# Stationary operands of a GRU scan interleaved in pairs, weight blocks displaced by some bytes

## Chip, cores and metric

The kernel runs on one core of a Trainium2 chip. The metric is the device time of one execution in microseconds, here the median of a few runs. Each profile is of one execution.

## The reference

Two stages, each added to its input. The first is a GRU over 64 steps (batch 128, width 512) followed by a linear layer with ternary weights; the second is a causal convolution and a mixture of experts. The change touches the first, which is

```python
def cell(h, x):
    gi = x @ W_ih + b_ih
    gh = h @ W_hh + b_hh
    i_r, i_z, i_n = jnp.split(gi, 3, axis=-1)
    h_r, h_z, h_n = jnp.split(gh, 3, axis=-1)
    r = jax.nn.sigmoid(i_r + h_r)
    z = jax.nn.sigmoid(i_z + h_z)
    n = jnp.tanh(i_n + r * h_n)
    h_new = (1.0 - z) * n + z * h
    return (h_new, h_new)
...
x = x + linear(scan(cell, cond_2048, x), ternary(weight)) + bias
x = x + moe(causal_conv(x, cond_2048) + b)
```

All inputs and outputs are float32.

## The kernel before

Time steps run one after the other. In each, x and h (128 rows of batch by 512) lie transposed: four k tiles of 128 features by 128 rows of batch. A product with a 512 x 512 block of weights is four matmuls that add up in one bank of PSUM: the k tile of x or h is the **stationary** operand (128 columns, loaded by an LDWEIGHTS of its own), and the four rows of the weight block (512 columns each) are the **moving** one. `products` (L337) issues such four.

To keep float32's precision with the faster type float32r, each operand is split in three: a part `h` with the low bits cut off, the rest `l`, and a mixture `s`. So one gate takes three products: h with h, l with l into one bank, s with s into another. Tiles of x are called xh, xl, xs, those of the state hh, hl, hs; the weights wih0 to wih2 and whh0 to whh2 (gates r, z, n), each in three planes; sgn is the ternary weight of the linear layer, multiplied with hh and hl only. In a settled step there are therefore 9 groups of four for x, 9 for h and 2 for sgn: 80 matmuls, and 4 transposes of h.

The order on TensorE in a step: wih2 and wih0 of the next step's x, the four transposes of h (`turned_up`, L418), wih1 of x, then the state's groups whh0h, whh2h, whh0l, whh0s, whh2l, whh2s, whh1 (three), then sgn for the state before.

The splitting: `masked` (L349) cuts the low bits on VectorE into `cut` (hcut from PSUM, xcut from SBUF), ScalarE casts it to the part h (L380, L436), and `low_parts` (L354) makes l (GpSimd for x from step 4 on, else VectorE) and s (VectorE). `late_ffn` (L563) does the same for four early steps whose linear layer is put off. Between them VectorE and ScalarE compute the gates (`cell_r`, `cell_n`, `cell_z`).

Memory: pools on the left grow from the low end (edge with `scale`, el0 with the tiles of x, wh0 to wh2 with whh, sgn), pools on the right from the high end (few, wi with wih, xp with the tiles of h). `scale` and `few` are made larger than needed by LEFT_PAD and RIGHT_PAD (in words of 4 bytes). By their sizes, all float32r tiles of the scan then begin at the same place modulo 1024 bytes.

Of the kernel before, what the change touches and what calls it, by code (L numbers as in the profile page):

```python
# [8 lines left out]
F32 = mybir.dt.float32  # L9
# [3 lines left out]
F32R = mybir.dt.float32r  # L13
# [6 lines left out]
P = 128  # L20
B = 128
T = 64
D = 512
KD = D // P
# [11 lines left out]
SPLIT = 4096.0  # L36
LOW = -4096
WHOLE = 1.0 + 1.0 / SPLIT
LEFT_PAD = 216
RIGHT_PAD = 504  # L40
DOWN_PAD = 216


# [5 lines left out]
def adaln_ffn_kernel(  # L49
# [22 lines left out]
    nc = tc.nc  # L72
# [51 lines left out]
    def clear(i):  # L124
        nc.gpsimd.memset(tzs[i], 0.0)
# [86 lines left out]
    with (  # L212
# [7 lines left out]
        br, bz, bin_, bhn, fb = (w0.tile([P, D], F32, name=n) for n in ("br", "bz", "bin", "bhn", "fb"))  # L220
        scale = edge.tile([P, LEFT_PAD], F32, name="scale")[:, :1]

        wi_ = ExitStack()
        few = wi_.enter_context(tc.tile_pool(name="few", bufs=1, side="right")).tile(
            [P, RIGHT_PAD], F32, name="few"
        )
        ones, part = few[:, :P], few[:, P : P + T]
        total, half, nhalf = (few[:, n : n + 1] for n in range(P + T, P + T + 3))
        wi = wi_.enter_context(tc.tile_pool(name="wi", bufs=1, side="right"))
        xpp = wi_.enter_context(tc.tile_pool(name="xp", bufs=2, side="right"))  # L230

        def planes(pool, name):
            return [pool.tile([P, KD, D], F32R, name=f"{name}{n}") for n in "hls"]

        wih = [planes(wi, f"wih{c}") for c in range(3)]
        wh0 = ExitStack()
        whh = [planes(wh0.enter_context(tc.tile_pool(name="wh0", bufs=1)), "whh0"), None, None]

        stage = ExitStack()
        st = stage.enter_context(tc.tile_pool(name="st", bufs=1))  # L240
# [12 lines left out]
        xps, xns, parts_of = {}, {}, {}  # L253
# [6 lines left out]
        LATE = 4  # L260
# [15 lines left out]
        def load_for(step):  # L276

            load_x(step - 1)
            t = postponed.get(step)
            if t is not None:  # L280
                load_x(t)
                hts[t] = slot()
                nc.gpsimd.dma_start(out=hts[t], in_=htd[t])
# [17 lines left out]
        h = el0.tile([P, D], F32, name="h")  # L301
# [25 lines left out]
        ps = ps_f.tile([P, D], F32, name="psf")  # L327
# [5 lines left out]
        def banks(c):  # L333
            pool = ps_gh if c == 1 else ps_gi
            return [pool.tile([P, D], F32, name=n) for n in BANKS[c]]

        def products(ps, lhs, rhs, start=False, stop=False):  # L337
            for k in range(KD):
                i = nc.tensor.matmul(  # L339
                    ps,  # L340
                    lhs[:, k, :],
                    rhs[:, k, :],
                    start=start and k == 0,
                    stop=stop and k == KD - 1,
                    skip_group_check=True,
                )
            return i

        def masked(dst, src):  # L349
            return nc.vector.tensor_scalar(  # L350
                dst.bitcast(I32), src.bitcast(I32), LOW, None, ALU.bitwise_and
            )

        def low_parts(engine, lo, mix, full, cut):  # L354

            i = engine.tensor_sub(lo, full, cut)  # L356
            nc.vector.scalar_tensor_tensor(mix, lo.bitcast(F32), -SPLIT, cut, ALU.mult, ALU.add)  # L357
            return i

# [13 lines left out]
        def split_x(t):  # L373

            xp = xps.pop(t)
            cut = xpp.tile([P, KD, B], F32, name="xcut", bufs=1)
            parts_of[t] = [el0.tile([P, KD, B], F32R, name=f"x{n}") for n in "hls"]
            xh, xl, xs = parts_of[t]
            masked(cut, xp)
            nc.scalar.copy(xh, cut)  # L380
            return low_parts(nc.vector if t < LATE else nc.gpsimd, xl, xs, xp, cut)

        gis = {}

# [40 lines left out]
        def place(t, n):  # L425

            if t < T - TAIL:
                return xpp.tile([P, KD, B], F32R, name=f"h{n}", bufs=1)
            return el0.tile([P, KD, B], F32R, name=f"x{n}")

        def split_h(ps, t, mixed=True):

            cut = el0.tile([P, KD, B], F32, name="hcut")
            hh, hl, hs = (place(t, n) for n in "hls")
            masked(cut, ps)
            nc.scalar.copy(hh, cut)  # L436
            if mixed:
                low_parts(nc.vector, hl, hs, ps, cut)
            else:
                nc.vector.tensor_sub(hl, ps, cut)  # L440
            return hh, hl, hs

        last = []
# [39 lines left out]
        def cell_r(t, ps):  # L483
            a, b = ps
            r = el0.tile([P, D], F32, name="rz")
            if t == 0:
                nc.vector.tensor_add(r, b, br)
            else:
                nc.vector.scalar_tensor_tensor(r, a, WHOLE, br, ALU.mult, ALU.add)
                nc.vector.tensor_add(r, b, r)  # L490
            nc.scalar.activation(r, r, AF.Sigmoid)  # L491
            return r
# [29 lines left out]
        for c in (0, 2, 1):  # L522
            a, b = banks(c)
# [14 lines left out]
        r = cell_r(0, first[0])  # L538
        n = cell_n(0, (None, first[2][1]), r)
# [23 lines left out]
        def late_ffn(t):  # L563

            hh, hl = (place(t, n) for n in "hl")
            cut = el0.tile([P, KD, B], F32, name="hcut")
            full = hts.pop(t).rearrange("p (k b) -> p k b", k=KD)
            masked(cut, full)
            nc.scalar.copy(hh, cut)
            nc.vector.tensor_sub(hl, full, cut)  # L570
            ffn(t, (hh, hl))

        split_x(1)
# [8 lines left out]
        for t in range(1, T):  # L582
            if t > LATE and t + 2 <= T:
                load_for(t + 2)
            if t + 2 < T:
                load_xt(t + 2)
            if 2 <= t < 2 * NSL + 2:
                toeplitz(t - 2)

            gates = [state_gate(t, c, pieces, hT) for c in (0, 2, 1)]  # L590
            next(gates[0])
            next(gates[1])
            ps_r, ps_n = next(gates[0]), next(gates[1])
            next(gates[2])
            ps_z = next(gates[2])
            if t + 1 < T:
                last_low = split_x(t + 1)
            if t > LATE:
                add_bias(t + 1, last_low)
            r = cell_r(t, ps_r)  # L600
            n = cell_n(t, ps_n, r)
            cell_z(t, ps_z, n)
            if t == LATE:
                ternary(wf)
                more.append(wi.tile([P, KD, D], F32, name="q"))
                for n in range(1, 3):
                    load_for(t + n)
                add_bias(t + 1)
            if t > LATE:
                ffn(t - 1, pieces)  # L610
            if t + 1 < T:
                pieces, hT = next_inputs(t)
            if t in (1, 2):
                c = 3 - t
                whh[c] = planes(
                    wh0.enter_context(tc.tile_pool(name=f"wh{c}", bufs=1, reuse_waits="tile")),
                    f"whh{c}",
                )
                with tc.tile_pool(name="cuts", bufs=2, reuse_waits="tile") as cuts:
                    convert(raw_h[c], whh[c], cuts)  # L620
                if t == 1:
                    late_.close()
                else:
                    sgn = wh0.enter_context(
                        tc.tile_pool(name="sgn", bufs=1, reuse_waits="tile")
                    ).tile([P, KD, D], F32R, name="sgn")
                    wf = wi.tile([P, KD, D], F32, name="q")
                    load_rows(wf, wfT)
            if t == T - TAIL:
                wi_.close()  # L630
                cb = conv.enter_context(
                    tc.tile_pool(name="cb", bufs=1, side="right", reuse_waits="tile")
                ).tile([P, D], F32, name="cb")
                for i in range(NCB):
                    conv_buffers(i)
                    clear(i)
                tail = conv.enter_context(
                    tc.tile_pool(name="tail", bufs=1, side="right", reuse_waits="tile")
                )
                xl = tail.tile([P, TAIL, D], F32, name="xl")  # L640
                tap = tail.tile([P, TAIL, D], F32, name="tap")
                load_piece(0)
                repeated(cb, cbias)
                for i in range(1, NCB):
                    load_piece(i)
                for j in range(TAIL):
                    nc.gpsimd.dma_start(out=tap[:, j], in_=cond[B - 1 - j].partition_broadcast(P))
                last += [xl, tap]
# [31 lines left out]
    xl, tap = last  # L680
# [19 lines left out]
    with tc.tile_pool(name="ps_c", bufs=4, space=PSUM) as ps_c:  # L700
        for sl in range(NSL):
# [6 lines left out]
            for g in range(DS // 4):  # L708
                if early:
                    ps = early.pop(0)  # L710
                else:
                    ps = conv_group(sl, g, ps_c.tile([P, D], F32, name="psc"))
# [33 lines left out]
    full = SI // P  # L746
# [963 lines left out]
    for i in range(NI // 2 + 1, NI):  # L1710
        n = i - NI // 2 - 1
# [64 lines left out]
```

## Time and profile before

| | us |
|---|---|
| median of 3 runs | 2439.01 (2437.75 to 2439.14) |
| the profiled execution | 2436.07 |
| its span, first to last instruction | 2434.0 |
| TensorE busy | 2420.9 (99%) |
| weight loads busy | 1866.9 (77%) |
| VectorE busy | 1579.1 (65%) |
| mean granted TensorE clock | 1.000 |

PE is TensorE's matmuls, PEld its weight loads, which overlap them; DVE is VectorE, ACT ScalarE, POOL GpSimd, SP the queue of SyncE. A timeline's line gives start and length in us, engine, line of the kernel, operation, result and inputs by the program's names, shapes (a moving operand of float32r is shown as f32 like any other) and how many instructions were merged; in brackets stands the idle time of the engine ahead of it and what ended it. Lengths of matmuls include their way through the array, so that consecutive ones overlap: the pace is read from the starts. Lines of groups give, behind the first bar, the busy time in us and the mean of one instruction in ns, and behind the second the engine's idle time ahead of them and what ended it.

The scan takes about the first 1207 us of the span. A settled step takes 18.63 us, from one set of transposes (start 505.55) to the next.

### The profile page before, as it was taken

To read this page: it belongs to the slowest core of one execution; us is meant where nothing else is said; L and a number is where in the kernel's file an instruction comes from. 1 tells how busy PE (TensorE), PEld (TensorE's weight loads), DVE (VectorE), ACT (ScalarE), POOL (GpSimd) and SP (SyncE) were. 2 spreads that over 40 slices of the span, in tenths; PEclk is the share of its full clock that TensorE was granted. 3 is DMA by queue.
4 is the path that set the end of the run, shared out by engine and by line. 5 is a ranking of instruction groups with operands and counts; after the bars stand their busy time and mean duration, and the time that the engine had idled before them with its cause. 6 is when DMAs were issued, how large, how long until landed. Compare 5 with 4: busy or idle time off the path is not lost.

```text
span 2434.0 us, 32114 instructions
## 1 busy us (share of the span) xinstructions
PE 2420.9 (99%) x12221; PEld 1866.9 (77%) x12221; DVE 1579.1 (65%) x3116; ACT 492.7 (20%) x900; POOL 447.2 (18%) x468
## 2 busy tenths in 40 slices
PE   9999999999999999999999999999999999999999
PEld 5788888888888888888896777777776666676667
DVE  8977777777777777777687766666753333343344
ACT  5211111111111111111123333233311111111111
POOL 1222221121112111211220000000012222222220
PEclk9999999999999999999999999999999999999999
DMA  5244443333232222222498123343459999899961
GB/s 188 80 85 82 80 81 59 67 66 63 57 61 57 57 54 59 60 53 48 130 344 291 29 40 75 98 113 92 135 147 288 296 297 304 268 321 307 286 180 34
DMA packets 469096, 330.71 MB, mean 136 GB/s; under 512 B 317136, under 2 KB 384720, under 8 KB 466768
## 3 DMA queue, kind: packets, MB, share of 16 engines
q1 hardware_dynamic: 439904, 254.47, 36.9%
q0 software_dynamic: 28896, 73.95, 12.9%
q8 instruction: 96, 1.57, 0.3%
q14 instruction: 56, 0.46, 0.1%
q10 hardware_dynamic: 144, 0.26, 0.0%
HBM read 241.83 MB, written 92.03 MB: 137 GB/s over the span
## 4 chain that ended last, share of the span: by engine, by line
PE 97%; DVE 1%; DMA 1%; issue 1%; ACT 0%; POOL 0%; DVEq 0%; ACTq 0%; POOLq 0%
PE psa L339 9%; PE psw L339 9%; PE psx L339 9%; PE psw L830 7%; PE psz L830 7%; PE psx L830 7%; PE psb L339 5%; PE psz L339 5%; PE psy L339 5%; PE psf L339 5%; PE py L1661 3%; PE y L830 3%; PE pg L1635 3%; PE pu L1635 3%; PE y L1006 2%; PE y L1098 2%
## 5 line engine op out<-in xcount | busy, mean ns | idle before, releaser
L1645 DVE SCALAR_TENSOR_TENSOR a<-a,rw,pu 128x352 f32<-128x352 f32 x32 | 18.6, 580 | 213.1 <-PE pu L1635 213.1
L357 DVE SCALAR_TENSOR_TENSOR xs<-xl,xcut 128x512 fp32r<-128x512 f32 x63 | 103.4, 1641 | 65.6 <-POOL xl L356 65.6
L1193 POOL DMA_DIRECT2D out_dram<-hid x60 | 53.4, 1075 | 493.5 <-DVE hid L1125 372.0
L830 PE MATMUL psx<-hid,sw 128*128 128x256 f32 x512 | 132.3, 381 | 0.0
L350 DVE TENSOR_SCALAR hcut<-pst 128x512 int32<-128x512 int32 x63 | 43.5, 691 | 130.1 <-PE pst L422 128.4
L356 POOL TENSOR_TENSOR xl<-xp,xcut 128x512 fp32r<-128x512 f32 x60 | 83.3, 1389 | 144.6 <-PE psa L339 131.7
L491 ACT ACTIVATE rz<-rz 128x512 f32<-128x512 f32 x64 | 40.5, 633 | 334.1 <-DVE rz L490 333.1
L830 PEld LDWEIGHTS psx<-hid,sw 128*128 128x128 f32 x512 | 94.3, 190 | 15.3 <-issue 2.9
L436 ACT CAST hh<-hcut 128x512 fp32r<-128x512 f32 x61 | 37.9, 621 | 325.0 <-DVE hcut L350 325.0
L272 POOL DMA_DIRECT2D q<-in_x_dram x36 | 19.3, 537 | 410.1 <-DMA out_dram<-q 328.1
L1661 PE MATMUL py<-wd,aeT 128*64 128x512 f32 (+1 forms) x288 | 88.7, 595 | 0.0
L830 PE MATMUL psw<-hid,st 128*128 128x256 f32 x320 | 83.1, 382 | 0.1
L1635 PE MATMUL pg<-wg,hid 128*64 128x352 f32 x384 | 81.1, 459 | 0.0
L1635 PE MATMUL pu<-wu,hid 128*64 128x352 f32 x384 | 81.1, 459 | 0.0
L1672 POOL DMA_INDIRECT out_dram<-hid,idxp x32 | 46.4, 1449 | 179.6 <-DMA out_dram<-hid,idxo 92.3
L1672 POOL DMA_INDIRECT out_dram<-hid,idxo x32 | 45.4, 1418 | 172.3 <-DMA out_dram<-hid,idxp 152.2
L870 ACT ACTIVATE g<-psx 128x256 f32<-128x256 f32 x80 | 30.8, 384 | 218.4 <-DVE aT L877 157.5
L504 ACT ACTIVATE n<-n 128x512 f32<-128x512 f32 x64 | 40.5, 633 | 166.6 <-DVE n L503 166.6
L339 PE MATMUL psa<-wih1h,xh 128*128 128x512 f32 x252 | 74.2, 415 | 0.0
L830 PE MATMUL y<-hid,st 128*128 128x256 f32 x280 | 74.0, 381 | 0.0
L272 POOL DMA_DIRECT2D xn<-in_x_dram x28 | 15.0, 537 | 318.6 <-DMA out_dram<-xn 269.5
L830 PE MATMUL psz<-hid,st 128*128 128x256 f32 x280 | 72.4, 380 | 0.0
(432 smaller groups left out, 6214.6 us busy)
## 6 DMA issues: line engine op xcount, KB each, us to landing
wg<-in_w_gate_dram SPq DMA_DIRECT2D x48, 704.0 KB, 12.7
wu<-in_w_up_dram SPq DMA_DIRECT2D x48, 704.0 KB, 13.4
wd<-in_w_down_dram SPq DMA_DIRECT2D x48, 512.0 KB, 10.8
xc<-x1c SPq DMA_DIRECT2D x32, 512.0 KB, 6.1
xp<-in_xT_dram POOLq DMA_DIRECT2D x62, 256.0 KB, 2.9
out_dram<-hid POOLq DMA_DIRECT2D x60, 256.0 KB, 5.2
tab<-hid SPq DMA_DIRECT2D x56, 256.0 KB, 5.0
hid<-in_w_gate_dram SPq DMA_DIRECT2D x16, 704.0 KB, 8.7
```

The lines of the kernel that those rows point to most:

```text
L339: i = nc.tensor.matmul(ps, lhs[:, k, :], rhs[:, k, :], start=start and k == 0, stop=stop and k == KD - 1, skip_group_check=True,)
L350: return nc.vector.tensor_scalar(dst.bitcast(I32), src.bitcast(I32), LOW, None, ALU.bitwise_and)
L356: i = engine.tensor_sub(lo, full, cut)
L357: nc.vector.scalar_tensor_tensor(mix, lo.bitcast(F32), -SPLIT, cut, ALU.mult, ALU.add)
L491: nc.scalar.activation(r, r, AF.Sigmoid)
L830: i = nc.tensor.matmul(ps.rearrange("p (j b) -> p j b", b=P) if len(r.shape) == 3 else ps, lhs(k), r, start=(first and k == 0), stop=(k == ...
L1006: nc.tensor.matmul(gu.rearrange("p (j b) -> p j b", b=P), swr[:, k].rearrange("p w n -> p (w n)"), rows[:, k], start=(k == 0), stop=(k == ...
L1098: nc.tensor.matmul(ps, aparts[n][:, c, steps], dparts[n][:, c], start=c == 0 and n != 1, stop=c == full - 1 and n != 0, skip_group_check=True,
L1193: nc.gpsimd.dma_start(out=out_t[t], in_=rows_of(i)[:, t % NB], accum_op=ALU.add)
L1635: nc.tensor.matmul(acc[halves[j]], self.xeT[:, k, halves[j]], self.ws[j][which][:, k, :], start=(k == 0), stop=(k == KD - 1),)
L1661: nc.tensor.matmul(py[halves[j]], self.aeT[:n, c, halves[j]], self.ws[j][2][:n, c, :], start=(c == 0), stop=(c == len(ech) - 1),)
L1672: nc.gpsimd.indirect_dma_start(out=out, out_offset=bass.IndirectOffsetOnAxis(ap=(idxp[:CAP] if j == 0 else idxo)[:, q : q + 1], axis=0), i ...
```

## The change

Tiles of x, of h and of their cuts are declared as 128 x 2 x 128 x 2 in place of 128 x 4 x 128: tiles k = 0 and 1 lie interleaved, column by column, and so do 2 and 3. A stationary operand's 128 columns are then 8 bytes apart, in place of 4. `apart` gives the view in the old order for writing, and `like` gives a plain source the same four dimensions. What reads and writes interleaved tiles only (the cast, the mixture) stays contiguous.

Unused tiles are placed between the weight blocks: 32 bytes behind wih0, 64 behind wih1, 160 behind wih2, and 64 ahead of each of whh0, whh2, whh1 and sgn. LEFT_PAD and RIGHT_PAD shrink by 64 words, the sum of these on each side.

```diff
-LEFT_PAD = 216
-RIGHT_PAD = 504
+LEFT_PAD = 152
+RIGHT_PAD = 440
...
-        wih = [planes(wi, f"wih{c}") for c in range(3)]
+        def shift(pool, name, words):
+            pool.tile([P, words], F32, name=name)
+
+        wih = []
+        for c, words in enumerate((8, 16, 40)):
+            wih.append(planes(wi, f"wih{c}"))
+            shift(wi, f"gap{c}", words)
         wh0 = ExitStack()
-        whh = [planes(wh0.enter_context(tc.tile_pool(name="wh0", bufs=1)), "whh0"), None, None]
+        wh0p = wh0.enter_context(tc.tile_pool(name="wh0", bufs=1))
+        shift(wh0p, "gap", 16)
+        whh = [planes(wh0p, "whh0"), None, None]
...
+        def paired(pool, name, dtype=F32R, **kw):
+
+            return pool.tile([P, KD // 2, B, 2], dtype, name=name, **kw)
+
+        def apart(pair):
+            return pair.rearrange("p m b r -> p m r b")
+
+        def like(ap):
+            return ap.rearrange("p (m r) b -> p m r b", r=2)
+
         def products(ps, lhs, rhs, start=False, stop=False):
             for k in range(KD):
                 i = nc.tensor.matmul(
                     ps,
-                    lhs[:, k, :],
+                    lhs[:, k, :] if len(lhs.shape) == 3 else lhs[:, k // 2, :, k % 2],
                     rhs[:, k, :],
...
-            i = engine.tensor_sub(lo, full, cut)
+            i = engine.tensor_sub(apart(lo), full, apart(cut))
             nc.vector.scalar_tensor_tensor(mix, lo.bitcast(F32), -SPLIT, cut, ALU.mult, ALU.add)
...
-            cut = xpp.tile([P, KD, B], F32, name="xcut", bufs=1)
-            parts_of[t] = [el0.tile([P, KD, B], F32R, name=f"x{n}") for n in "hls"]
+            cut = paired(xpp, "xcut", F32, bufs=1)
+            parts_of[t] = [paired(el0, f"x{n}") for n in "hls"]
             xh, xl, xs = parts_of[t]
-            masked(cut, xp)
+            masked(apart(cut), like(xp))
             nc.scalar.copy(xh, cut)
...
                 c = 3 - t
-                whh[c] = planes(
-                    wh0.enter_context(tc.tile_pool(name=f"wh{c}", bufs=1, reuse_waits="tile")),
-                    f"whh{c}",
-                )
+                whp = wh0.enter_context(
+                    tc.tile_pool(name=f"wh{c}", bufs=1, reuse_waits="tile")
+                )
+                shift(whp, "gap", 16)
+                whh[c] = planes(whp, f"whh{c}")
```

`place`, `split_h` and `late_ffn` get the same rewriting as `split_x`, and sgn a gap of 16 words in its pool.

More of the change, by code (lines that the diff above doesn't have):

```diff
@@ L375, in split_x @@
             xp = xps.pop(t)
-            cut = xpp.tile([P, KD, B], F32, name="xcut", bufs=1)
-            parts_of[t] = [el0.tile([P, KD, B], F32R, name=f"x{n}") for n in "hls"]
+            cut = paired(xpp, "xcut", F32, bufs=1)
+            parts_of[t] = [paired(el0, f"x{n}") for n in "hls"]
             xh, xl, xs = parts_of[t]
-            masked(cut, xp)
+            masked(apart(cut), like(xp))
             nc.scalar.copy(xh, cut)
-            return low_parts(nc.vector if t < LATE else nc.gpsimd, xl, xs, xp, cut)
+            return low_parts(nc.vector if t < LATE else nc.gpsimd, xl, xs, like(xp), cut)
         gis = {}
@@ L427, in place @@
             if t < T - TAIL:
-                return xpp.tile([P, KD, B], F32R, name=f"h{n}", bufs=1)
-            return el0.tile([P, KD, B], F32R, name=f"x{n}")
+                return paired(xpp, f"h{n}", bufs=1)
+            return paired(el0, f"x{n}")
         def split_h(ps, t, mixed=True):
-            cut = el0.tile([P, KD, B], F32, name="hcut")
+            cut = paired(el0, "hcut", F32)
             hh, hl, hs = (place(t, n) for n in "hls")
-            masked(cut, ps)
+            masked(apart(cut), like(ps))
             nc.scalar.copy(hh, cut)
             if mixed:
-                low_parts(nc.vector, hl, hs, ps, cut)
+                low_parts(nc.vector, hl, hs, like(ps), cut)
             else:
-                nc.vector.tensor_sub(hl, ps, cut)
+                nc.vector.tensor_sub(apart(hl), like(ps), apart(cut))
             return hh, hl, hs
@@ L565, in late_ffn @@
             hh, hl = (place(t, n) for n in "hl")
-            cut = el0.tile([P, KD, B], F32, name="hcut")
+            cut = paired(el0, "hcut", F32)
             full = hts.pop(t).rearrange("p (k b) -> p k b", k=KD)
-            masked(cut, full)
+            masked(apart(cut), like(full))
             nc.scalar.copy(hh, cut)
-            nc.vector.tensor_sub(hl, full, cut)
+            nc.vector.tensor_sub(apart(hl), like(full), apart(cut))
             ffn(t, (hh, hl))
@@ L623, in adaln_ffn_kernel @@
                 else:
-                    sgn = wh0.enter_context(
+                    sgp = wh0.enter_context(
                         tc.tile_pool(name="sgn", bufs=1, reuse_waits="tile")
-                    ).tile([P, KD, D], F32R, name="sgn")
+                    )
+                    shift(sgp, "gap", 16)
+                    sgn = sgp.tile([P, KD, D], F32R, name="sgn")
                     wf = wi.tile([P, KD, D], F32, name="q")
```

## The prediction

> **What bounds the kernel now.** I read the page first, then the weight loads and matmuls one shape apart, then the timeline of one step of the scan, then the timeline of a later stage for comparison. The page:
>
> ```profile
> PE 2420.9 (99%) x12221; PEld 1866.9 (77%) x12221; DVE 1579.1 (65%) x3116; ACT 492.7 (20%) x900; POOL 447.2 (18%) x468
> ...
> PE 97%; DVE 1%; DMA 1%; issue 1%; ACT 0%; POOL 0%; DVEq 0%; ACTq 0%; POOLq 0%
> ```
>
> TensorE is never free and owns 97% of the chain that ended last, so only its pace counts. The timeline of one step, in start and length (us):
>
> ```profile
> 506.19 0.69 DVE L350 TENSOR_SCALAR hcut<-pst 128x512 int32<-128x512 int32 x1 [2.41 <-PE pst L422]
> ...
> 506.91 0.62 ACT L436 CAST hh<-hcut 128x512 fp32r<-128x512 f32 x1 [6.21 <-DVE hcut L350]
> 506.91 0.69 DVE L356 TENSOR_TENSOR hl<-pst,hcut 128x512 fp32r<-128x512 f32 x1
> ...
> 508.53 0.87 PEld L339 LDWEIGHTS psx<-whh0h,hh 128*128 128x128 f32 x4
> 508.76 1.07 PE L339 MATMUL psx<-whh0h,hh 128*128 128x512 f32 x4
> ...
> 510.35 0.87 PEld L339 LDWEIGHTS psx<-whh0l,hl 128*128 128x128 f32 x4
> ```
>
> And ten groups later in the same step, and in the late stage at 2003 us:
>
> ```profile
> 518.73 1.07 PE L339 MATMUL psw<-wih2h,xh 128*128 128x512 f32 x4
> ```
>
> ```profile
> 2003.42 1.03 PE L830 MATMUL psx<-hid,sw0first 128*128 128x256 f32 x4
> 2004.28 1.03 PE L830 MATMUL y<-hid,st 128*128 128x256 f32 x4
> 2005.15 0.49 PE L1650 MATMUL py<-ident,a 128*128 128x128 f32 x3
> ```
>
> From start 508.76 to start 518.73 lie 44 matmuls: 226.6 ns from one to the next. From 2003.42 to 2005.15 lie 8: 216.3 ns. The first kind (float32r, 512 columns) and the second (float32, 256 columns, taking twice the time for a column) keep the array busy for the same number of column times, and the granted clock is 1.0 in both. So the scan's matmuls lose 10.3 ns each that the others don't.
>
> **What the two kinds differ in.** Each matmul runs beside the weight load of the next:
>
> ```profile
> L194 PEld LDWEIGHTS psc<-tz,xc 128*64 128x64 f32 x960 | 55.7, 200 | 2.8 <-issue 2.8
> ...
> L339 PEld LDWEIGHTS psx<-whh0l,hl 128*128 128x128 f32 x244 | 45.8, 188 | 9.5
> ...
> L1239 PEld LDWEIGHTS lg<-hid,gw 128*64 128x64 f32 x256 | 17.8, 137 | 11.1 <-issue 2.8 <-DVE hid L1225 0.3
> ```
>
> The last number ahead of the second bar is the mean of one load. Contiguous loads take 137 ns for 64 columns and 188 for 128: 51 ns for 64 more, 102 ns for the 128. A load therefore reads its 512 bytes of a partition at some 5.0 bytes/ns. The float32 matmul reads 1024 bytes in 216 ns, 4.7 bytes/ns: nearly equal speeds, no loss. The float32r matmul reads 2048 bytes in that time, 9.5 bytes/ns, so the two read streams slide past each other, and this kind loses. I infer that the two streams get in each other's way in the memory when one overtakes the other; no row shows it directly.
>
> **The change, part by part.**
>
> *Interleaving the stationary columns.* A load now spreads 128 columns over 1024 bytes: at 102 ns, 10 bytes/ns, the speed of the moving stream. If what is lost comes from sliding, it goes. The pace in the changed state is in no row, so I bound it: below by the float32 row, 216.3 ns; above by charging the 10.3 ns to the 16-byte pieces that a load touches, 32 now and 64 then: 20.6 ns lost, 236.9. I take 218, near the equal-speed row, leaving 1.7 ns for the start of each load. The float32r matmuls of L339 whose stationary operand changes are nine groups of 252, six of 244, three of 240 and two of 248: 4948. At 226.6 - 218 = 8.6 ns each this is 42.6 us. At the bounds: -51.0 us and +51.0 us.
>
> *The load itself.* If strided columns load more slowly, it may no longer hide. The only strided row is L194, 64 bytes apart: 63 ns more for 64 columns. Doubled for 128 that is 126 ns more, 228 ns of reading instead of 102, which would set a pace of 228: 1.4 x 4948 = 7 us lost. At 8 bytes two columns share a 16-byte piece, so half of the extra, 63 ns, is the nearer estimate: 165 ns of reading, still inside 216. I take nothing.
>
> The Trainium skill, "SBUF — State Buffer", Specifications, asks for at least two hits on each 16-byte line for full bandwidth; 8 bytes gives exactly two. Its page "TensorE: Matmul & The Clock Gate", Step-by-step, speaks against the change: loading the next weights is said not to steal read bandwidth from the running matmul, as the two have separate ports. By that nothing would be gained and the sum would stay at 2439; the 226.6 against 216.3 above does not fit it.
>
> *Displaced weight blocks.* Against the stationary tiles, and counted modulo 256 bytes, the moving blocks now begin 0 (wih0, sgn), 32 (wih1), 64 (whh0), 96 (wih2), 128 (whh2) and 192 bytes (whh1) further; before, all began at the same place. With equal speeds this distance stays fixed through a load, so it may decide. No row shows another distance. Of the 80 matmuls in a step 20 (12 of wih0, 8 of sgn) have distance 0; if only those collide, at +10.3 ns, and the rest gain 10.3, the sum is 4948 x 10.3 x (60 - 20)/80 = 25 us gained.
>
> *The first matmuls behind the transposes.* From 505.90 to 508.76 twelve matmuls take 2.86 us, 0.14 more than 12 x 226.6; some 0.09 of it is the first pair of loads. The other 0.05 x 62 steps = 3 us: I take 2 of them.
>
> *Splitting with strides.* Per step VectorE's hcut, hl, xcut, GpSimd's xl read or write with an 8-byte step. A strided write costs VectorE nothing in the row of L715 (418 ns for 256 elements in short runs, against 423 for the contiguous L864), and the casts and mixes stay contiguous. The cover: hh is done at 507.53 and its first load starts at 508.53, 1.0 us; hl is done at 507.60 for a load at 510.35, 2.7 us. If hcut doubled (0.69 us) it would still be hidden; if hcut and the cast both doubled, hh would be 0.3 us late, 19 us over 61 steps. xcut (470 ns) may rise to hcut's 691; xl could double its 1389 ns: xs would be done near 512.9 and is first read some 8 us later. h itself is done 2.9 us before its transposes. I take nothing.
>
> *Issues.* No DMA, wait or semaphore is added or moved; total padding is the same.
>
> **Sum.** -42.6 - 2 = -44.6 us. The profiled execution took 2436.1 (span 2434.0 and 2 around it), 3 under the median of 2439.0; so 2391.5 for one like it, **2394** for the median.
>
> **The rivals.**
>
> 1. *Lines, not speeds* (slower). Each 16-byte piece that a load reads delays the moving stream, whatever the speeds. Twice the pieces, twice the loss: up to +51 us, 2490. For it: a load-time row that grows with the stride, 200 against 137. Against: the same pieces cost the float32 stages nothing, and L194, with a new piece in every column, still keeps its matmuls going. It decides once the mean pace in the scan exceeds 226.6 ns; half the bound gives 2465.
> 2. *Some distances collide* (partly faster). 2414 as worked out above, at wih0 and sgn.
> 3. *The change doesn't do what it says.* The 10.3 ns belongs to float32r itself, and layout is nothing to it: 2439. For it: the same 226.6 in every group of the scan. Against: behind the transposes the pace varies without a change of the data type.
>
> **How the numbers follow.** Forecast 0.40 (own range 2380 to 2405), rival 2 0.16, rival 3 0.06, rival 1 0.38. A measurement here tells about 0.2% (5 us) from no change. Faster 0.56, same 0.06, slower 0.38. The range runs from 2380, just under the lower bound (2439 - 51 - 3 = 2385), up to 2470, which takes in all but the worse half of rival 1.
>
> **What would show it.** In the timeline of a step, starts of the L339 groups 0.87 us apart (right), 0.91 (rival 3), 0.95 (rival 1), or different from block to block (rival 2); the step 17.8 us from transposes to transposes instead of 18.63; the weight-load row of L339 at 188 to 250 ns; hcut and hl at 0.69 us. I would be wrong altogether if loads stopped hiding, seen as gaps on TensorE ahead of L339, or if hh came late.

## The result

| | before | after |
|---|---|---|
| median of 4 runs, us | 2438.38 | 2464.01 (2461.48 to 2464.95) |
| ratio of the times | | 1.0103, interval 1.0091 to 1.0116 |
| the profiled execution, us | 2436.07 | 2463.17 |
| its span, us | 2434.0 | 2461.3 |

The changed kernel is slower by 25.6 us, where 44.6 us less had been forecast. The page of the changed kernel, its busy times and its chain:

```profile
PE 2448.1 (99%) x12221; PEld 1905.9 (77%) x12221; DVE 1582.5 (64%) x3116; ACT 492.1 (20%) x900; POOL 447.5 (18%) x468
...
PE 97%; DVE 1%; DMA 1%; issue 1%; ACT 0%; POOL 0%; DVEq 0%; ACTq 0%; POOLq 0%
```

TensorE is still the whole chain (97%) and never free; it is busy 27 us longer for the same 12221 instructions. The timeline of one settled step of the changed kernel, TensorE alone:

```profile
612.30 0.60 PE L440 MATMUL pst<-ident,h 128*128 128x128 f32 x4
612.66 1.19 PE L357 MATMUL psa<-wih1h,xh 128*128 128x512 f32 x4
...
615.56 1.10 PE L357 MATMUL psx<-whh0h,hh 128*128 128x512 f32 x4
...
625.77 1.09 PE L357 MATMUL psw<-wih2h,xh 128*128 128x512 f32 x4
...
631.35 0.60 PE L440 MATMUL pst<-ident,h 128*128 128x128 f32 x4
```

From the transposes at 612.30 to those at 631.35 lie 19.05 us, against 18.62 before. From 615.56 to 625.77 lie 44 matmuls, 232.0 ns from one to the next where it was 226.6. The 57 steps behind the first six take 1092.9 us against 1069.1 (sums over the starts of the transposes), 23.8 of the 27.3 us by which the two spans differ; the first steps hold 2.9 more. So nearly all of the loss is the pace of the float32r matmuls. Rows of the work that was costed at nothing, and of a load, in the changed kernel:

```profile
L374 POOL TENSOR_TENSOR xl<-xp,xcut 128x512 fp32r<-128x512 f32 x60 | 84.1, 1402 | 157.0 <-PE psa L357 143.9 <-issue 12.9
...
L357 PEld LDWEIGHTS psx<-whh0l,hl 128*128 128x128 f32 x244 | 47.7, 196 | 9.2
...
L368 DVE TENSOR_SCALAR hcut<-pst 128x512 int32<-128x512 int32 x63 | 43.5, 691 | 138.1 <-PE pst L440 135.8 <-ACT xn L574 2.3
...
L374 DVE TENSOR_TENSOR hl<-pst,hcut 128x512 fp32r<-128x512 f32 x61 | 42.2, 691 | 2.0
...
L368 DVE TENSOR_SCALAR xcut<-xp 128x512 int32<-128x512 int32 x63 | 29.7, 471 | 5.2
```

hcut and hl take the 691 ns of before, xcut 471 for 470, GpSimd's xl 1402 for 1389: reading and writing 8 bytes apart cost next to nothing in this kernel. A load takes 196 ns for 188.

Behind the mean stands another picture than before. The distance from one start to the next, in ns, for the four k tiles of a group (mean over the settled steps):

```
                    before               changed kernel
psx<-whh0h,hh       227 227 227 227      232 235 232 232
psw<-whh2h,hh       227 227 227 227      229 236 229 233
psx<-whh0l,hl       227 227 227 227      233 235 230 236
psa<-whh1l,hl       227 227 227 227      228 230 233 229
psw<-wih2h,xh       227 227 227 227      227 234 234 235
```

Before, one number for every group. After, numbers from 227 to 236 that differ from matmul to matmul and return in every step within 1 to 3 ns. The steady pace is gone; nothing has come near 216.

### The profile page after: what moved, and what is told of

Read it like the earlier page. It is cut to its first block, busy times and chain, and to the rows that moved or that the text cites. A ratio compares the mean times of both kernels' runs of the same rounds, so it can differ in the third digit from the quotient of the medians.

```text
span 2461.3 us, 32114 instructions
## 1 busy us (share of the span) xinstructions
PE 2448.1 (99%) x12221; PEld 1905.9 (77%) x12221; DVE 1582.5 (64%) x3116; ACT 492.1 (20%) x900; POOL 447.5 (18%) x468
## 4 chain that ended last, share of the span: by engine, by line
PE 97%; DVE 1%; DMA 1%; issue 1%; ACT 0%; POOL 0%; DVEq 0%; ACTq 0%; POOLq 0%
PE psx L357 9%; PE psw L357 9%; PE psa L357 9%; PE psw L851 7%; PE psz L851 7%; PE psx L851 7%; PE psb L357 5%; PE psz L357 5%; PE psy L357 5%; PE psf L357 5%; PE py L1682 3%; PE y L851 3%; PE pg L1656 3%; PE pu L1656 3%; PE y L1027 2%; PE y L1119 2%
## 5 line engine op out<-in xcount | busy, mean ns | idle before, releaser
L374 POOL TENSOR_TENSOR xl<-xp,xcut 128x512 fp32r<-128x512 f32 x60 | 84.1, 1402 | 157.0 <-PE psa L357 143.9
```

The source lines that it names most:

```text
L374: i = engine.tensor_sub(apart(lo), full, apart(cut))
```

## The experiments

The pace lost 10.3 ns against 216 before the change and some 16 after it. The expectations weigh theories of where this comes from; in words: that it is the load's reading (the pieces it touches, or its duration), that the distance between the places where the two streams start decides, and that the moving stream loses by itself, whatever the load reads (called D where it is tested). Seven runs take the change apart, alter the loads or move the tiles; the other seven alter what the matmul streams. Times are set beside the kernel before on the same chip; those without an interval are of one run each.

### Half of the change at a time

The interleaving alone, with the padding of before, so that all tiles begin together:

```diff
-LEFT_PAD = 152
-RIGHT_PAD = 440
+LEFT_PAD = 216
+RIGHT_PAD = 504
...
         def shift(pool, name, words):
-            pool.tile([P, words], F32, name=name)
+            return
```

> Interleaved columns (8 bytes apart), padding and weight blocks as before. Theory A (the displacement took away the common start of all blocks, and with it the steady pace of 226.6 ns; the interleaving by itself costs nothing): pace 226.6 ns, 2439 us. Theory B (the doubled number of 16-byte pieces in a load costs the extra 6 ns, wherever the blocks lie): pace 232 to 233 ns in every block, 2464 us. Theory C (equal speeds help, but only at one distance): pace 216 to 218, about 2390.

Measured: 2471.23 us, ratio 1.0132 (1.0116 to 1.0149). The matmuls start 234 ns apart in the mean, in a pattern of three that goes through all groups: 233, 233 and 234 ns in some steps, 233, 235 and 239 in others.

The displacements alone, columns contiguous as before:

```diff
         def paired(pool, name, dtype=F32R, **kw):
-            return pool.tile([P, KD // 2, B, 2], dtype, name=name, **kw)
+            return pool.tile([P, KD, B], dtype, name=name, **kw)
         def apart(pair):
-            return pair.rearrange("p m b r -> p m r b")
+            return pair
         def like(ap):
-            return ap.rearrange("p (m r) b -> p m r b", r=2)
+            return ap
```

> Columns 4 bytes apart as before, weight blocks displaced as in the change. Theory A: pace 232 to 233 ns, 2464 us. Theory B: pace 226.6, 2439 us. If pace depends on the distance, it differs between wih0, wih1, wih2, whh0, whh2, whh1 and sgn.

Measured: 2459.32 us, ratio 1.0086 (1.0069 to 1.0103). Each half alone takes the steady pace away, and together they lose less (25.6 us) than the interleaving alone (33); the parts don't add up. Neither theory A nor theory B stands: each expected one of the halves to keep 226.6 ns. The timeline of the displaced kernel:

```profile
606.47 1.10 PE L357 MATMUL psz<-wih2s,xs 128*128 128x512 f32 x4
607.41 1.09 PE L357 MATMUL psx<-wih0h,xh 128*128 128x512 f32 x4
...
613.40 1.07 PE L357 MATMUL psx<-whh0h,hh 128*128 128x512 f32 x4
614.31 1.08 PE L357 MATMUL psw<-whh2h,hh 128*128 128x512 f32 x4
```

From its start to the next, wih2s takes 0.94 us for its four matmuls (235 ns each) and whh0h 0.91 (227): the pace differs from block to block. A block's distance alone doesn't set it, though: wih0, at distance 0, takes 231, 232 and 228 ns in its three groups (means over the settled steps).

All four k tiles interleaved, so that columns lie 16 bytes apart, a new 16-byte piece each:

```diff
-            return pool.tile([P, KD // 2, B, 2], dtype, name=name, **kw)
+            return pool.tile([P, 1, B, KD], dtype, name=name, **kw)
...
-            return ap.rearrange("p (m r) b -> p m r b", r=2)
+            return ap.rearrange("p (m r) b -> p m r b", r=KD)
...
-                    lhs[:, k, :] if len(lhs.shape) == 3 else lhs[:, k // 2, :, k % 2],
+                    lhs[:, k, :] if len(lhs.shape) == 3 else lhs[:, 0, :, k],
```

> All four k tiles interleaved: columns 16 bytes apart, one in each 16-byte piece, blocks as before. Theory A: no change from the kernel with pairs alone. Theory B: loss again doubled against pairs, pace 240 to 250 ns, 2500 to 2550 us. Loads themselves, 188 ns before, at 200 to 310 ns.

Measured: 2488.01 us, ratio 1.0204 (1.0187 to 1.0221). The load's row of this kernel:

```profile
L357 PEld LDWEIGHTS psx<-whh0l,hl 128*128 128x128 f32 x244 | 62.3, 311 | 0.4
```

A load now lasts 311 ns (the mean behind the first bar; loads that follow each other overlap in the profile) and the weight loads have no idle time left (0.4 us over 244 of them), so that here they may set the pace themselves. Yet matmuls still start 230 to 240 ns apart, 235.3 in the mean, against 234.1 with pairs: a load that lasts 1.6 times as long adds 1.2 ns. The rest of its time is the first matmul behind the transposes, where such a load is not hidden (440 ns to the next start, against 324), and the first steps. VectorE's hcut rises to 1.10 us here, still hidden.

### The stationary side

Every load reads one column 128 times: a partition's 512 bytes become 4, in one piece.

```diff
-                    lhs[:, k, :],
+                    lhs[:, k, 0:1].to_broadcast([P, B]) if lhs.dtype == F32R else lhs[:, k, :],
```

> Every float32r weight load of the scan reads one column 128 times (step 0), so it touches one 16-byte piece in place of 32; the products are then not the reference's. Both theories hold that reads of the loads cost the matmuls 10.3 ns: pace 216 to 217 ns, 2439 - 52 = 2387 us. If the pace stays 226.6, the loss does not come from what a load reads.

Measured: 2455.44 us, ratio 1.0068 (1.0051 to 1.0085). The timeline of this kernel, ten groups apart:

```profile
611.38 1.08 PE L339 MATMUL psx<-whh0h,hh 128*128 128x512 f32 x4
...
620.62 1.09 PE L339 MATMUL psf<-sgn,hl 128*128 128x512 f32 x4
```

9.24 us for 40 matmuls, 231 ns each. 216 had been expected, and the loss grew instead. So it doesn't go away when a load reads one piece in place of 32, and 4 bytes in place of 512; and the steady 226.6 was lost.

Loads of 64 columns in the products with xl and hl:

```diff
-        def products(ps, lhs, rhs, start=False, stop=False):
+        def products(ps, lhs, rhs, start=False, stop=False, m=P):
...
-                    ps,
-                    lhs[:, k, :],
+                    ps[:m],
+                    lhs[:, k, :m],
```

> Kernel before with 64 in place of 128 stationary columns in the groups of xl, hl and sgn with hl, so that their loads read for half the time; the upper 64 rows of those products are left out. If the 10.3 ns are lost for as long as a load reads: matmuls beside such a load at 221 to 222 ns, the rest at 226.6 or a little off, 2439 - 7 x 4 x 62 x 5 ns = 2430 us. If a load costs a fixed amount or nothing: 226.6 everywhere.

Measured: 2449.72 us against 2436.62. Three groups of it:

```profile
611.65 1.09 PE L339 MATMUL psy<-whh0s,hs 128*128 128x512 f32 x4
612.58 1.08 PE L339 MATMUL psw<-whh2l,hl 128*64 128x512 f32 x4
613.50 1.09 PE L339 MATMUL psz<-whh2s,hs 128*128 128x512 f32 x4
```

The group with 64 columns (128*64) takes 0.92 us to the next start, the full one ahead of it 0.93; before, both took 0.91. Loads of 135 ns in place of 188 lose no less, where 221 to 222 ns had been expected if the loss lasted as long as the load reads.

Everything moved by 64 bytes, so that all still begin together, and then the tiles on the left (x, whh, sgn) moved by 128 against those on the right (h, wih), so that every pair starts 128 bytes apart:

```diff
-LEFT_PAD = 216
-RIGHT_PAD = 504
+LEFT_PAD = 232
+RIGHT_PAD = 488
```

```diff
-LEFT_PAD = 216
+LEFT_PAD = 184
```

> Columns 4 bytes apart, no gaps; all float32r tiles of the scan, stationary and moving, begin 64 bytes further, so every distance between the two stays 0. If the distance sets the pace: 226.6 ns, 2439 us. If the absolute position does (a start on a multiple of 1024 bytes): 229 to 233 ns, 2450 to 2465 us.

> Columns 4 bytes apart, no gaps; all tiles on the left begin 128 bytes lower, so every block has the same distance of 128 bytes, and nothing changes it within a step. If a steady pace needs equal distances from block to block: a steady pace is found behind the transposes as before, at 226.6 ns or another value, and 2439 us for 226.6. If it needs the distance 0: 231 to 234 ns throughout, 2460 to 2470 us. A steady pace under 224 ns would beat the kernel before.

Measured: 2436.44 us for the first, with 226.6 ns as before; 2465.64 for the second, against 2436.62. Two groups of the second:

```profile
608.28 1.10 PE L339 MATMUL psw<-wih2l,xl 128*128 128x512 f32 x4
609.21 1.10 PE L339 MATMUL psz<-wih2s,xs 128*128 128x512 f32 x4
```

The first takes 0.93 us to the next start, 233 ns a matmul; one by one they start 237, 229, 238 and 229 ns apart in turn, in nearly every block alike. So not the place, but the distance between the starts of the two streams decides whether the steady pace is found. It isn't the spread of distances in the change that hurts; one distance that isn't zero does the same. And in the groups shown the rows of wih lie where they lay before, and of the two operands only x has moved: what is lost depends also on where the load reads. Distance 0 isn't enough by itself: the interleaving alone and the loads of 64 columns have it too, and their matmuls take 234 and 230 ns in the mean.

### The moving side

The matmul streams its first column 512 times:

```diff
-                    rhs[:, k, :],
+                    rhs[:, k, 0:1].to_broadcast([P, D]) if lhs.dtype == F32R else rhs[:, k, :],
```

> Kernel before with the moving operand of every float32r matmul of the scan read from one column (step 0); the products are then not the reference's. If the loss comes from the moving stream and the load meeting in the memory over a range of addresses: pace 216 to 218 ns, about 2387 us. If the loss is there whatever is read: 226 to 235 ns.

Measured: 2384.15 us against 2436.62. The timeline, eight groups apart:

```profile
613.83 1.03 PE L339 MATMUL psx<-whh0h,hh 128*128 128x512 f32 x4
...
620.73 1.03 PE L339 MATMUL psb<-whh1s,hs 128*128 128x512 f32 x4
```

6.90 us for 32 matmuls, 215.6 ns each: with the loads untouched (188 to 192 ns), all of the 10.3 ns is gone. This is the mirror image of the run with one column in the load: the loss needs a moving stream that goes through its row, and no load that goes through its columns.

How much of the row must be read for the loss to come? The first n columns, repeated: 4 for wih2, 16 for wih0, 64 for wih1, 128 for whh0 and whh2, 256 for whh1.

```diff
+        def moving(row, n):
+            return row[:, :n].unsqueeze(1).to_broadcast([P, D // n, n]) if n else row
...
-                    rhs[:, k, :],
+                    moving(rhs[:, k, :], n),
```

> Kernel before, but a moving row of 512 columns reads only its first n columns, over and over: n = 4 (16 bytes) in wih2, 16 (64 bytes) in wih0, 64 (256 bytes) in wih1, 128 (512 bytes) in whh0 and whh2, 256 (1024 bytes) in whh1, all 512 in sgn; the products are then not the reference's. Theory D (the moving stream loses time by itself, on each new piece of memory): 216 ns at the smallest ranges and 227 to 236 from some range on, whatever the loads do. Theory E (it loses where it meets the load's range of 512 bytes): 216 only where it hardly moves, and a loss that grows with the range up to 512 bytes.

Measured: 2439.53 us against 2436.03. The timeline:

```profile
611.79 1.07 PE L344 MATMUL psf<-sgn,hl 128*128 128x512 f32 x4
612.69 1.03 PE L344 MATMUL psw<-wih2h,xh 128*128 128x512 f32 x4
613.56 1.03 PE L344 MATMUL psw<-wih2l,xl 128*128 128x512 f32 x4
...
615.28 1.13 PE L344 MATMUL psx<-wih0h,xh 128*128 128x512 f32 x4
616.25 1.14 PE L344 MATMUL psx<-wih0l,xl 128*128 128x512 f32 x4
```

wih2, 16 bytes over and over, takes 0.87 us for four (216 ns each in the mean). wih0, 64 bytes over and over, takes 0.97 (242), worse than sgn with its whole rows, 0.90 (226). The blocks with 512 bytes and more keep 227, and wih1 with 256 settles there. So nothing is lost within 16 bytes and the most at 64; a longer range adds nothing, and the growth up to 512 bytes that theory E expected isn't found.

And in which order? The row in n equal parts, one column of each in turn: n = 2 for wih2, 4 for wih0, 8 for wih1, 16 for whh0 and whh2, 128 for whh1 (every column 16 bytes behind the last).

```diff
+        def moving(row, n):
+            return row.rearrange("p (r m) -> p m r", r=n) if n else row
```

> Kernel before, but a moving row is read in another order: in n parts, one column from each in turn, n = 2 in wih2, 4 in wih0, 8 in wih1, 16 in whh0 and whh2, 128 in whh1 (every column 16 bytes behind the last), contiguous in sgn; the products are then not the reference's. If a new 16-byte piece costs the stream time: the pace worsens to well above 236 ns wherever neighbours lie apart, most at 128. If the order is free, 224 to 237 everywhere. A block at 216 to 220 would show an order that loses nothing.

Measured: 3150.56 us against 2436.03. The timeline:

```profile
604.04 2.15 PE L344 MATMUL psa<-wih1l,xl 128*128 128x512 f32 x4
605.99 2.15 PE L344 MATMUL psb<-wih1s,xs 128*128 128x512 f32 x4
607.93 1.94 PE L344 MATMUL psx<-whh0h,hh 128*128 128x512 f32 x4
609.68 1.93 PE L344 MATMUL psw<-whh2h,hh 128*128 128x512 f32 x4
...
618.38 2.04 PE L344 MATMUL psa<-whh1h,hh 128*128 128x512 f32 x4
620.23 2.04 PE L344 MATMUL psa<-whh1l,hl 128*128 128x512 f32 x4
...
625.82 1.02 PE L344 MATMUL psw<-wih2h,xh 128*128 128x512 f32 x4
626.68 1.03 PE L344 MATMUL psw<-wih2l,xl 128*128 128x512 f32 x4
...
629.53 1.30 PE L344 MATMUL psx<-wih0l,xl 128*128 128x512 f32 x4
630.66 1.30 PE L344 MATMUL psy<-wih0s,xs 128*128 128x512 f32 x4
```

Eight parts: 1.95 us for four matmuls, 487 ns each. Sixteen: 1.75 us, 437. 128: 1.85 us, 462. Four parts: 1.13 us, 283. But two parts: 0.86 us, 216 in the mean, all of the loss gone. The worst is eight, not 128 as expected. The distance from one part to the next changes with their number, from 1024 bytes for two to 16 for 128, so that these five numbers don't tell which of the two sets the price.

### Reading in turn from two halves

Two parts can be had for whole products: the weight planes and sgn are stored with a row's even columns first and its odd columns behind them, and the matmul reads the two halves in turn, so that its columns come in the old order.

```diff
+        def halves_of(row):
+            return row.rearrange("p (r m) -> p r m", r=2)
+        def even_odd(row):
+            return row.rearrange("p (m r) -> p r m", r=2)
+        def in_turn(row):
+            return row.rearrange("p (r m) -> p m r", r=2)
...
-                    rhs[:, k, :],
+                    in_turn(rhs[:, k, :]) if lhs.dtype == F32R else rhs[:, k, :],
...
-                masked(cut, raw[:, k])
+                masked(halves_of(cut), even_odd(raw[:, k]))
...
-                nc.vector.tensor_sub(lo, raw[:, k], cut)
+                nc.vector.tensor_sub(halves_of(lo), even_odd(raw[:, k]), halves_of(cut))
```

(and likewise where sgn is made). Once in the kernel before, and once in the changed kernel, with its interleaving and its displacements:

> Kernel before, complete and with the reference's products: weight planes and sgn are stored with even columns first, and a moving row is read in turn from its two halves (1024 bytes apart), which gives the natural order again. Theory D (the moving stream alone loses the time, and not in this order): 216 ns in every block, some 2384 us. If the 216 of wih2 in the last run came from something else in that kernel: 226 to 237 ns.

> The changed kernel with the same storing and reading of the moving rows. If interleaving and displacement cost only through the moving stream (theory D): 216 ns in every block, 2384 us, as without them, and the change's 25 us are gone. If the loads' 64 pieces or the distances cost by themselves (theories B and C): some 6 ns a matmul more than in the kernel before read in the same way, 2410 us.

Measured: 2384.82 us, ratio 0.9782 (0.9768 to 0.9795), and 2385.11, ratio 0.9782 (0.9767 to 0.9797). The timeline of the second:

```profile
610.49 0.60 PE L449 MATMUL pst<-ident,h 128*128 128x128 f32 x4
...
613.53 1.03 PE L366 MATMUL psx<-whh0h,hh 128*128 128x512 f32 x4
...
623.02 1.03 PE L366 MATMUL psw<-wih2h,xh 128*128 128x512 f32 x4
```

From 613.53 to 623.02 lie 44 matmuls, 215.7 ns each, with the transposes some 17.7 us apart instead of 19.05. With the moving stream read in turn, the change's 25.6 us are gone to within the intervals: stationary layout and distances are then indifferent. The change costs only through a moving stream that is read contiguously.

VectorE's strided work isn't free in this kernel, though it stays hidden:

```profile
L383 DVE TENSOR_TENSOR hl<-pst,hcut 128x512 fp32r<-128x512 f32 x61 | 51.7, 848 | 2.0
...
L377 DVE TENSOR_SCALAR hcut<-pst 128x512 int32<-128x512 int32 x63 | 50.1, 796 | 99.7 <-PE pst L449 98.3 <-ACT xn L590 1.4
```

hl takes 848 ns and hcut 796, where both took 691 in the changed kernel (the same 8-byte steps, the row contiguous) and take 691 and 690 in the kernel before when its rows are read in turn (steps of 4 bytes). Both together raise them; why isn't shown.

Also in the later stage, whose products with split weights are float32r too (420 matmuls):

```diff
-                                dparts[n][:, c],
+                                in_turn(dparts[n][:, c]),
```

> As the first of these three, and the 420 float32r matmuls of the shared expert's down products (L1098 of the kernel before), at 227 ns there, read in turn too: 420 x 10.6 = 4.5 us less, and up to 2 more behind the float32 groups; 2378 to 2380 us.

Measured: 2377.20 us (2376.47 to 2378.41), ratio 0.9752 (0.9738 to 0.9765), the fastest of all, 61 us below the kernel before. Its page begins:

```profile
PE 2359.2 (99%) x12221; PEld 1876.7 (79%) x12221; DVE 1575.2 (66%) x3116; ACT 492.1 (21%) x900; POOL 450.8 (19%) x468
```

TensorE's busy time is 62 us below that of before with the same instructions. Against the previous version it gains 7.6 us; 420 x 10.6 ns would be 4.5. Of the 7.2 us between the two profiled executions 4.6 lie behind the last transposes of the scan, where the later stage is, and 2.6 in the first steps of the scan, whose code is the same in both.

Last, whether the two places must lie far apart. Neighbouring pieces in turn, of 16 bytes (wih2), 32 (wih0), 64 (wih1), 256 (whh0, whh2) and 512 (whh1); sgn contiguous, as a measure:

```diff
+        def moving(row, n):
+            return row.rearrange("p (q r m) -> p q m r", r=2, m=n) if n else row
```

> Kernel before, but a moving row is read in turn, one column each, from two neighbouring pieces of n columns, then from the next two: pieces of 16 bytes in wih2, 32 in wih0, 64 in wih1, 256 in whh0 and whh2, 512 in whh1, contiguous in sgn; the products are then not the reference's. If reading in turn from any two pieces loses nothing: 216 ns in every block but sgn. If the two pieces must lie far apart: 216 ns from some distance on, and 227 ns or more under it.

Measured: 2386.46 us against 2436.70. The timeline:

```profile
604.69 1.08 PE L344 MATMUL psf<-sgn,hh 128*128 128x512 f32 x4
605.61 1.07 PE L344 MATMUL psf<-sgn,hl 128*128 128x512 f32 x4
606.51 1.03 PE L344 MATMUL psw<-wih2h,xh 128*128 128x512 f32 x4
607.38 1.03 PE L344 MATMUL psw<-wih2l,xl 128*128 128x512 f32 x4
...
614.72 1.03 PE L344 MATMUL psx<-whh0h,hh 128*128 128x512 f32 x4
615.59 1.03 PE L344 MATMUL psw<-whh2h,hh 128*128 128x512 f32 x4
```

sgn takes 0.92 and 0.90 us for its four; the other blocks settle at 0.86 to 0.87. Every pair of pieces tried will do, down to neighbours 16 bytes long.

## Why the prediction was wrong

**The step that failed** is "What the two kinds differ in": the inference that the 10.3 ns come from the load's stream and the moving stream sliding past each other, on which "Interleaving the stationary columns" put equal speeds and a pace of 218. The speeds did become nearly equal (a load lasts 196 ns in place of 188 and spreads over twice the bytes), and the interleaving alone gave 234 ns. In its place the runs show that the loss hangs on the moving row being read contiguously: with the load cut to one piece it stays (231 ns), with the moving stream cut to one piece it goes (216), and with that stream read in turn from two pieces it goes as well (216), in the layout before and in the changed one. In the sum, the term of -42.6 us came out as some +33 by itself, and +25.6 together with the displacement.

Not shown is that the load has no part in it. Every matmul here has a load beside it, and moving x by 128 bytes, with the rows of wih in their place, took the steady 226.6 away: a meeting of the two streams that the reading in turn avoids remains possible. Nor is it shown why float32 lies at 216; equal speeds alone don't bring it about.

**The size of the price.** The forecast's upper bound, 236.9 ns for twice the pieces, was near the 232 measured, so that rival 1's time (2465 for half the bound) is the one measured. That is luck, as its mechanism fails: a load of a single piece costs as much as one of 64 (231 against 232). What the change removes is a steady state. At distance zero, with whole contiguous loads, the matmuls settle to 226.6 within some twelve of them; interleaved or displaced they settle elsewhere or not at all, at 232 to 235 in the mean.

**Displaced weight blocks.** "If only those collide", at distance 0, had it the wrong way round: zero is the only distance at which any run settled at 226.6. The displacement alone costs 21 us.

**Rival 3** came closest in cause (the loss belongs to how float32r streams), but held the layout to be nothing; layout sets how much of it comes.

**The first matmuls behind the transposes.** Two us were to be gained; the twelve take 2.90 us (612.66 to 615.56) where they took 2.86.

**What held.** That only TensorE's pace counts; that the loads stay hidden (196 ns, within the 188 to 250 named); that splitting is free in the changed kernel (691, 691 and 471 ns); that the bound for a pace of 216 is 51 us of gain: the run that streams one column gained 52.5, and reading in turn gained 53.4. For the load itself, the 63 ns taken as half of L194's extra came out as 8; the whole extra, 126 ns for a new piece in every column, came out as 123 (311 against 188).

**Rules against rows.** The Trainium skill, "TensorE: Matmul & The Clock Gate", Back-to-back issue gap, gives N/2.4 + 2.5 ns for an isolated matmul, 215.8 for 512 columns, and says that this counts too much for a stream of loads and matmuls. The kernels that read in turn agree with the formula (215.8 in the mean); the kernel before, at 226.6, does not, so that figure holds here only for some orders of reading, and in the settled steps of all runs no float32r matmul started less than 215 ns behind another. Its section Step-by-step, that a load doesn't steal read bandwidth, had been set aside in the prediction because of the 226.6. The run with one column fits it (a load of 4 bytes frees nothing); the run with 128 bytes between the two sides doesn't fit a load that leaves the matmul alone. "SBUF — State Buffer", Specifications, charges every access that goes to a new line. For 128 parts (a new line each time, 462 ns) that fits; for two lines in turn, where every access changes the line and nothing is lost (216), it doesn't.

**Still open.** Why distance zero between the starts lets the contiguous stream settle at 226.6, and why the load's layout moves its pace at all when the load's bytes don't cost: the runs show that both do, and not how. No run streams a row with no load beside it, which would tell whether the row loses by itself.

## What to carry to other kernels

A float32r matmul that streams a contiguous row need not run at its best pace, though TensorE shows as 99% busy: read the pace from starts, and compare it with another kind of matmul in the same profile. Reading the row in turn from two halves, with the columns stored to suit, took it from 226.6 to 216 ns here, 53 us of the kernel's time. And before a loss is put down to two parties that meet, make each of them trivial in turn; two such runs would have pointed at the moving row before any layout was designed.

## What the hardware showed unexpectedly

The order in which a matmul reads its moving float32r row decides its pace: 216 ns from two pieces in turn, 226.6 contiguous at best and up to 235 in the mean, 283 from four, 487 from eight, 437 from sixteen and 462 from 128. Small displacements of whole tiles change a kernel's time by 1%: 128 bytes between the two sides cost 29 us, 64 bytes of both together nothing. A load of 128 columns takes 188 ns at 4 bytes from column to column, 196 at 8 and 311 at 16. VectorE's hcut takes 691 ns at steps of 4 and 8 bytes and 1.10 us at 16; at 8 bytes, with TensorE reading in turn, 796.
